# Query projections without padding, score units that include the diagonal, and a new rule for the gaps

## The chip, the cores and the metric

The kernel runs on one core of one Trainium2 chip. The metric is the time of one execution on the device in microseconds (us); the median of several executions is given. Engines are named as in the profile: PE is TensorE (PEld its weight loads), DVE is VectorE, ACT is ScalarE, POOL is GpSimd, SP is SyncE, which here only issues transfers. L401 is line 401 of the kernel before.

## The reference

One transformer layer, all in float32, with x of shape (2, 1024, 256):

```
q = x @ Wq   (16 heads of 16)        k, v = x @ Wk, x @ Wv   (4 heads of 16, each for 4 query heads)
att = softmax(q k^T / 4 + slope * (key position - query position), causal)
x = layernorm(x + (att v) @ Wo)
shared = (silu(x @ shared_gate) * (x @ shared_up)) @ shared_down
routed = one of 8 experts per row (256 -> 2 x 512 -> 256), input scaled by sigmoid(top logit)
out = layernorm(x + shared + routed)
```

## The kernel before

Rows are cut into 16 tiles of 128, eight in each batch. The four key/value heads g lie in the four quadrants of 32 partitions: kT[b] holds for head g in its 32 rows a position row, a row of ones and, from row 16 of the quadrant on, the 16 values of the head. qT[b] has the same layout for the REP = 4 query heads of a group, one after another in the free dimension, so that one matmul of 32 rows gives scores with the position term in them. In the kernel before, Wq is padded for this (`wq_pad`, 4 x 32 columns for each r): `do_q(b, r, i)` multiplies half a batch (512 columns) by one padded block for each of two r, and ScalarE adds `qbias` (the slopes, in the position rows) while it copies the result (tile `qpj`) to qT (L341).

The work before the experts goes in four stretches.

1. Start: `first_projections` turns the first half of batch 0 by transposes (`xtp0`), then projects k and v (`do_kv`: tiles kpj and vpj) and q, and turns the second half (`turn_x`, tile xtp).
2. The lead: LEAD = 10 score units run ahead of the loop, and between them `projections` puts the k, v and q of the other three halves.
3. The loop over `steps`, one for each (batch, query tile qt, key tile kt) with kt <= qt. As long as score units are left, a step has two slots. In each slot, TensorE runs a burst of four interleaved tiles: two of "t" (`t_ps`, L485: transposed scores from which ScalarE makes the probabilities pT, pD) and two of "s" (`s_ps`, L401: scores from which VectorE takes the row maximum). Behind the burst comes a gap, in which `gap(room)` may place a product (`yT`, L529), the spread of the maxima (`mT`) and the next small pieces of a finished query tile (`finish`: yq, ytp, o_ps, x1tp, lg).
4. Steps without score units have one burst and a `wide_gap`, in which a piece of the shared expert (gu_sh, dp_sh) goes too; at the end a few `last_gap`s.

A score unit covers all four g in two halves h of two quadrants, with one tile of 512 columns for each g: nr query heads times n key tiles. `s_units` gives each query tile a unit of its own for the diagonal (four heads by one key tile, four matmuls of 128 columns for each g), and units of 4, 2 or 1 key tiles for the past. In `end_s`, VectorE reduces a past tile to its maximum (L417); of a diagonal unit, VectorE takes the minimum with a causal bound for one half (L427), while ScalarE copies the other half (L435), which GpSimd masks (L438). A later reduction (L449) takes the diagonal's maximum. `maxima` joins the maxima of a query tile three slots before its first step (`join_maxima`), and one slot later transposes them into the query rows (`spread_maxima`, qS, L474).

The tiles t_ps, s_ps and all projections share six PSUM banks (`ps_st`), the small pieces and mT have one (`ps_m`), yT one. The program's order on PE, DVE, ACT and POOL is as written; SP's queue is ordered by the scheduler in this part, and as written in the experts' part. SP's transfers before the attention: x, Wo, the router, then sh_gate, sh_up and sh_down (L110 to L112) and a fill of the experts' slots in DRAM (`slot_x`, L281, 3.9 MB). The experts follow; the diff leaves them alone except for the name of the set of engines.

Of the kernel before, what the change touches and what calls it, by code (L numbers as in the profile page):

```python
# [30 lines left out]
    mybir.EngineType.DVE,  # L31
    mybir.EngineType.Activation,
    mybir.EngineType.Pool,
}


# [8 lines left out]
def attn_moe_postln_kernel(  # L45
# [61 lines left out]

    sh_gu = const.tile([P, KC, F2], F32, tag="sh_gu", name="sh_gu")
    sh_d = const.tile([P, FC, C], F32, tag="sh_d", name="sh_d")
    nc.sync.dma_start(out=sh_gu[:, :, :FF], in_=sh_gate.rearrange("(c p) f -> p c f", p=P))  # L110
    nc.sync.dma_start(out=sh_gu[:, :, FF:], in_=sh_up.rearrange("(c p) f -> p c f", p=P))
    nc.sync.dma_start(out=sh_d, in_=sh_down.rearrange("(c p) n -> p c n", p=P))  # L112

# [9 lines left out]

    wq_pad = acon.tile([P, KC, REP, N_KV, PAD], F32, tag="wq_pad", name="wq_pad")
    wk_pad = acon.tile([P, KC, N_KV, PAD], F32, tag="wk_pad", name="wk_pad")
    nc.vector.memset(wk_pad, 0.0)  # L130
    nc.vector.memset(wq_pad, 0.0)
    for c in range(KC):
        nc.vector.tensor_scalar_mul(
            wq_pad[:, c, :, :, ROW_HEAD : ROW_HEAD + HD],
            wq_raw[:, c, :].rearrange("p (g r d) -> p r g d", g=N_KV, d=HD),
            scale,
        )
        nc.vector.tensor_copy(
            wk_pad[:, c, :, ROW_HEAD : ROW_HEAD + HD],
            wk_raw[:, c, :].rearrange("p (g d) -> p g d", d=HD),  # L140
        )
# [121 lines left out]
    with (  # L263
# [11 lines left out]
    ):  # L275
        qT, kT, xT = {}, {}, {}

        empty = shp.tile([P, ROW], F32, tag="th", name="empty")
        nc.gpsimd.memset(empty, 0.0)
        nc.gpsimd.memset(empty[:, NUM : NUM + 1].bitcast(I32), NTT * P)  # L280
        nc.sync.dma_start(out=slot_xt, in_=empty.unsqueeze(1).broadcast_to([P, SLOTS // P, ROW]))  # L281


        def pj_tile(name):
            return ps_m.tile([P, 512], F32, tag="m", name=name)
# [1 line left out]
        def own_tiles(b, xTb):  # L287
            xT[b] = xTb
            kT[b] = qkp.tile([P, T], F32, tag="kT", name=f"kT_{b}")
            qT[b] = qkp.tile([P, REP, T], F32, tag="qT", name=f"qT_{b}")  # L290

        def project(dst, b, w, cols):
            for c in range(KC):
                nc.tensor.matmul(  # L294
                    dst, lhsT=w(c), rhs=xT[b][:, c, cols], start=(c == 0), stop=(c == KC - 1)
                )

        def wq_of(r):
            return lambda c: wq_pad[:, c, r].rearrange("p g d -> p (g d)")

        def wk_of(c):
            return wk_pad[:, c].rearrange("p g d -> p (g d)")
# [5 lines left out]
        def turn_x(b, i):  # L308
            if b not in xT:

                xTb = ptp.tile([P, KC, T], F32, tag="pT", name=f"xT_{b}")
                own_tiles(b, xTb)
            for c in range(KC):
                tp = bank("xtp")
                for j in range(4):
                    nc.tensor.transpose(tp[:, ts(j, P)], xs[:, b * QT + i + j, ts(c, P)], ident)
                nc.scalar.copy(xT[b][:, c, i * P : (i + 4) * P], tp)
# [15 lines left out]
                    )  # L333
            nc.scalar.copy(vs[b][:, i : i + 4, :, 0:HD], pv)

        def do_q(b, r, i):
            cols = slice(i * P, (i + 4) * P)
            for j in range(2):
                pj = bank("qpj")
                project(pj, b, wq_of(r + j), cols)  # L340
                nc.scalar.activation(qT[b][:, r + j, cols], pj, AF.Identity, bias=qbias)  # L341

        halves = [(b, i) for b in range(B) for i in range(0, QT, 4)][1:]

        def projections():


            pieces = []
            for h, after in zip(halves, [*halves[1:], None]):
                pieces.append((11, lambda h=h: do_kv(*h)))  # L350
                pieces.append((14, lambda h=h: do_q(h[0], 0, h[1])))
                if after:
                    pieces.append((4, lambda h=after: turn_x(*h)))
                pieces.append((14, lambda h=h: do_q(h[0], 2, h[1])))
            return pieces

        def first_projections():

            own_tiles(0, xTp.tile([P, KC, T], F32, tag="xT", name="xT_0"))
            cols = slice(0, 512)  # L360
            warm = bank("warm")
            zeros = mnegs[0].rearrange("p r g d -> p (r g d)")
            for i in range(2):
                nc.tensor.matmul(warm, lhsT=zeros[:, :P], rhs=zeros, start=True, stop=True)
            for c, copy in enumerate((nc.scalar.copy, nc.vector.tensor_copy)):
                tp = bank("xtp0")
                for j in range(4):
                    nc.tensor.transpose(tp[:, ts(j, P)], xs[:, j, ts(c, P)], ident)
                copy(xT[0][:, c, cols], tp)
            do_kv(0, 0)  # L370
            do_q(0, 0, 0)
            do_q(0, 2, 0)
            turn_x(*halves[0])


        def s_units(b, qt):

            units = [(0, REP, qt, 1)]
            done = 0
            while done < qt:  # L380
                n = 4 if qt - done >= 4 else 2 if qt - done >= 2 else 1
                units += [(r, 4 // n, done, n) for r in range(0, REP, 4 // n)]
                done += n
            return [(b, qt, *u) for u in units]

# [2 lines left out]
        def start_s(unit, h, j):  # L388
            b, qt, r0, nr, key, n = unit
            if (b, qt) not in rowmax:  # L390
                rowmax[b, qt] = (
                    mp.tile([P, N_KV, REP, P], F32, tag="diag", name="diag"),
                    mp.tile([P, N_KV, REP, 4], F32, tag="past", name="past", bufs=6),
                )
                parts[b, qt] = {qt: 0}
            parts[b, qt].setdefault(key, len(parts[b, qt]))
            g = h * HALF + j
            rows = slice(g * PAD, (g + 1) * PAD)
            sp = bank("s_ps")
            return sp, [  # L400
                lambda r=r: nc.tensor.matmul(  # L401
                    sp[:, r * n * P : (r + 1) * n * P],
                    lhsT=qT[b][rows, r0 + r, ts(qt, P)],
                    rhs=kT[b][rows, key * P : (key + n) * P],
                    start=True,
                    stop=True,
                )
                for r in range(nr)
            ]

        def end_s(unit, h, sp, last):
            b, qt, r0, nr, key, n = unit
            diag, past = rowmax[b, qt]
            gs = slice(h * HALF, (h + 1) * HALF)
            if key != qt:
                for j in range(HALF):
                    nc.vector.tensor_reduce(  # L417
                        past[:, h * HALF + j, r0 : r0 + nr, parts[b, qt][key]],
                        sp[j].rearrange("p (r k) -> p r k", r=nr),
                        AX.X,  # L420
                        ALU.max,
                        negate=True,
                    )
                return
            if not last:
                for j in range(HALF):
                    nc.vector.tensor_tensor(  # L427
                        diag[:, h * HALF + j],
                        sp[j].rearrange("p (r k) -> p r k", r=REP),
                        causal.unsqueeze(1).broadcast_to([P, REP, P]),  # L430
                        ALU.min,
                    )
            else:
                for j in range(HALF):
                    nc.scalar.copy(  # L435
                        diag[:, h * HALF + j].rearrange("p r k -> p (r k)"), sp[j]
                    )
                nc.gpsimd.affine_select(  # L438
                    out=diag[:, gs],
                    in_=diag[:, gs],  # L440
# [335 lines left out]
        def maxima():  # L776
            n = 0
            for k in order:
                if slot == 2 * first[k] - 3:
                    join_maxima(*k)  # L780
                if slot == 2 * first[k] - 2:
                    spread_maxima(*k)
                    n += 1
            return n
# [10 lines left out]
        def gap(room):  # L795
            nonlocal slot
            after_burst()
            start_route(True)
            if products and products[0][0] <= slot:
                product(*products.pop(0)[1])  # L800
                room -= 4
            room -= 4 * maxima()
            pieces(room)
            slot += 1

        def wide_gap():
# [6 lines left out]
            if not maxima():  # L813
                pieces(4, 4)
            slot += 1
            if tail:
                tail.pop(0)()
            after_burst()
            if not maxima():
                pieces(4, 4)  # L820
            slot += 1
# [22 lines left out]
        for k in range(LEAD):  # L844
# [5 lines left out]
            while fill and left * LEAD > total * (LEAD - 1 - k):  # L850
                left -= fill[0][0]
                fill.pop(0)[1]()
            gap(0)
        for n, (b, qt, kt) in enumerate(steps):
            last = n + 1 == len(steps) or steps[n + 1][:2] != (b, qt)
            made = []
# [40 lines left out]
    with (  # L897
# [6 lines left out]
        tc.tile_pool(name="ps_d", bufs=2, space=PSUM) as ps_d,  # L904
        tc.tile_pool(name="ps_t", bufs=2, space=PSUM) as ps_t,
        tc.tile_pool(name="rt2", bufs=1) as rtp,
        tc.manual_schedule(engines=MANUAL | {mybir.EngineType.SP}),
    ):
        wgu = wgup.tile([P, E, KC, F2], F32, tag="wgu", name="wgu")
        wd = wgup.tile([P, E, FC, C], F32, tag="wd", name="wd")  # L910
# [386 lines left out]
```

## Time and profile before

| | us |
|---|---|
| median of 6 runs | 601.69 (600.35 to 604.02) |
| the profiled execution | 603.76 |
| its span, first to last instruction | 602.0 |
| TensorE busy | 574.7 |
| VectorE busy | 343.4 |
| ScalarE busy | 267.1 |
| GpSimd busy | 155.3 |
| s_ps matmuls, L401, 1280 instructions | 185.4 |
| t_ps matmuls, L485, 576 instructions | 175.1 |
| qpj matmuls, L294, 64 instructions | 29.1 |
| mean granted TensorE clock | 0.985 |

Every fp32 matmul of the program stands as two instructions in the profile (640 score matmuls are 1280 instructions). Busy time of a group is the union of its instructions, so the four interleaved tiles of a burst count once. Matmuls in different quadrants run side by side. In the views of stretches the columns are: the stretch, its length, then for PE, PEld, DVE, ACT and POOL the busy time with the number of instructions in brackets, the granted clock, the busy share of the DMA engines and their GB/s. In a line of groups, the numbers behind the bar are busy us, mean ns of one instruction, and idle us before them with what ended it. In a timeline, they are the start and the length in us. In a line of transfers they are the KB of each and the median us from issue to landing.

### The profile page before, as it was taken

Reading aid. Unit: us, or ns where it says so; the run is one execution under the profiler, and the core shown is the slowest. Engines: PE = TensorE matmul, PEld = TensorE weight load, DVE = VectorE, ACT = ScalarE, POOL = GpSimd, SP = SyncE. Lnnn points to the kernel's source line nnn. Section 1 sums busy time; section 2 is a strip of 40 time slices with the busy share of each in tenths; the row PEclk is TensorE's granted clock in tenths of the full one; section 3 lists DMA queues with packets and bytes.
Section 4 is the critical chain, followed back from the end, with each engine's and each line's share of the span. In section 5 each row is a group of like instructions: output and inputs, shape, how many; then the busy total and the mean of one; then the engine's idle time right before and its main releaser. Section 6 shows DMA issues by size and latency. Waiting matters only on the chain. (4 is left out here: it accounts for less than half of the span.)

```text
span 602.0 us, 9431 instructions
## 1 busy us (share of the span) xinstructions
PE 574.7 (95%) x3708; PEld 329.0 (55%) x3708; DVE 343.4 (57%) x734; ACT 267.1 (44%) x484; POOL 155.3 (26%) x189
## 2 busy tenths in 40 slices
PE   8999999999999999998999999999999999999990
PEld 4555535444445353434356644545664788888650
DVE  3186767867676767777767745332551264444541
ACT  1433466665665655646575755554112111111120
POOL 4010222111110102013321220232101237766541
PEclk9999979999999999999999999999999999999996
DMA  8800000000000000000100000110153545752100
GB/s 306 249 1 2 2 0 2 1 1 1 2 2 1 1 1 0 3 0 28 45 1 1 2 1 1 35 37 1 35 203 110 176 157 180 255 180 78 46 21 4
DMA packets 23105, 32.66 MB, mean 54 GB/s; under 512 B 3295, under 2 KB 18949, under 8 KB 23057
## 3 DMA queue, kind: packets, MB, share of 16 engines
q1 hardware_dynamic: 18784, 25.28, 12.7%
q0 software_dynamic: 3456, 6.34, 3.0%
q8 instruction: 31, 0.51, 0.4%
q10 hardware_dynamic: 816, 0.39, 0.2%
q14 instruction: 18, 0.14, 0.1%
HBM read 22.20 MB, written 12.97 MB: 58 GB/s over the span
## 5 line engine op out<-in xcount | busy, mean ns | idle before, releaser
L401 PE MATMUL s_ps<-kT,qT 32*128 32x128 f32 (+2 forms) x1280 | 185.4, 380 | 1.2 <-DVE past L417 0.7
L417 DVE TENSOR_REDUCE past<-s_ps 128x1 f32<-128x512 f32 (+2 forms) x224 | 144.6, 685 | 62.6 <-PE s_ps L401 46.0
L485 PE MATMUL t_ps<-qS,kT 32*128 32x512 f32 x576 | 175.1, 642 | 0.3 <-ACT pD L507 0.3
L504 ACT ACTIVATE pT<-t_ps 128x512 f32<-128x512 f32 x224 | 121.8, 600 | 93.7 <-PE s_ps L401 65.5
L401 PEld LDWEIGHTS s_ps<-kT,qT 32*128 32x128 f32 x1280 | 96.8, 185 | 14.4 <-ACT pT L504 4.5
L485 PEld LDWEIGHTS t_ps<-qS,kT 32*128 32x128 f32 x576 | 54.0, 184 | 63.4 <-issue 23.8
L509 POOL TENSOR_SCALAR_AFFINE_SELECT pD<-pD 128x1024 f32<-128x1024 f32 x32 | 34.8, 1093 | 102.8 <-ACT pD L507 102.6
L529 PE MATMUL yT<-pT,v 128*32 128x512 f32 x448 | 59.7, 605 | 0.0
L438 POOL TENSOR_SCALAR_AFFINE_SELECT diag<-diag 128x1024 f32<-128x1024 f32 x16 | 17.5, 1094 | 135.1 <-ACT diag L435 114.4
L233 POOL TENSOR_TENSOR rstd<-rstd,neg_half 128x1 f32<-128x1 f32 x36 | 20.6, 572 | 115.4 <-DVE rstd L232 113.0
L507 ACT COPY pD<-t_ps 128x512 f32<-128x512 f32 x64 | 34.7, 601 | 24.5 <-PE s_ps L401 13.9
L688 PE MATMUL gu_sh<-x1T,sh_gu 128*128 128x512 f32 x96 | 43.5, 596 | 0.0
L239 POOL DMA_INDIRECT slot_x<-xs,slots x32 | 32.1, 1004 | 42.1 <-DVE slots L669 24.3
L449 DVE TENSOR_REDUCE past<-diag 128x8 f32<-128x1024 f32 x32 | 38.6, 1210 | 0.0
L521 ACT ACTIVATE pD<-pD 128x1024 f32<-128x1024 f32 x32 | 33.9, 1065 | 0.2 <-POOL pD L509 0.2
L1116 ACT ACTIVATE sg<-gp 128x512 f32<-128x512 f32 x16 | 9.6, 597 | 54.6 <-PE gp L1108 54.6
L1108 PE MATMUL gp<-slot_xT,wgu 128*128 128x256 f32 x128 | 30.4, 381 | 1.2 <-ACT slot_xT L1077 1.2
L1108 PE MATMUL up<-slot_xT,wgu 128*128 128x256 f32 x128 | 30.2, 379 | 0.0
L294 PE MATMUL qpj<-xT,wq_pad 128*128 128x512 f32 x64 | 29.1, 600 | 0.1
L1124 PE MATMUL dp<-wd,slot_h 128*128 128x256 f32 x128 | 29.0, 379 | 0.0
L427 DVE TENSOR_TENSOR diag<-s_ps,causal 128x512 f32<-128x512 f32 x32 | 20.5, 683 | 13.9 <-PE s_ps L401 13.9
L1053 POOL DMA_INDIRECT zt<-z_dram,row x20 | 20.7, 1033 | 27.8 <-issue 27.5
(170 smaller groups left out, 665.9 us busy)
## 6 DMA issues: line engine op xcount, KB each, us to landing
wgu<-_L_ffn_gate_up_proj_dram SPq DMA_DIRECT2D x8, 1024.0 KB, 8.8
wd<-in_L_ffn_down_proj_dram SPq DMA_DIRECT2D x8, 512.0 KB, 5.8
slot_x<-empty SPq DMA_DIRECT2D x1, 3900.0 KB
row<-slot_x SPq DMA_DIRECT2D x8, 260.0 KB, 2.9
xs<-in_L_attn_x_dram SPq DMA_DIRECT2D x4, 512.0 KB, 8.1
z_dram<-z_sh SPq DMA_DIRECT2D x12, 128.0 KB, 1.8
row<-slot_x SPq DMA_DIRECT2D x4, 130.0 KB, 2.0
sh_gu<-L_ffn_shared_gate_w_dram SPq DMA_DIRECT2D x1, 512.0 KB
```

What stands on the lines that cost most here:

```text
L239: inst = nc.gpsimd.indirect_dma_start(out=to, out_offset=bass.IndirectOffsetOnAxis(ap=index, axis=0), in_=rows, in_offset=None, bounds_che ...
L401: lambda r=r: nc.tensor.matmul(sp[:, r * n * P : (r + 1) * n * P], lhsT=qT[b][rows, r0 + r, ts(qt, P)], rhs=kT[b][rows, key * P : (key + n ...
L417: nc.vector.tensor_reduce(past[:, h * HALF + j, r0 : r0 + nr, parts[b, qt][key]], sp[j].rearrange("p (r k) -> p r k", r=nr), AX.X, ALU.max ...
L449: lambda: nc.vector.tensor_reduce(past[:, gs, :, 0], diag[:, gs], AX.X, ALU.max, negate=True),
L485: lambda: nc.tensor.matmul(tp, lhsT=kT[b][rows, ts(kt, P)], rhs=qS[b, qt][rows].rearrange("p r q -> p (r q)"), start=True, stop=True,)
L504: nc.scalar.activation(p[:, j], tp[j], AF.Exp)
L507: nc.scalar.copy(p[:, j], tp[j])
L509: nc.gpsimd.affine_select(out=p, in_=p, pattern=[[0, HALF * REP], [1, P]], compare_op=ALU.is_ge, fill=MASKED, base=0, channel_multiplier=-1,)
L521: lambda: nc.scalar.activation(p, p, AF.Exp),
L529: nc.tensor.matmul(yTs[b, qt][g * PAD : (g + 1) * PAD], lhsT=vs[b][:, kt, g, :], rhs=p[:, g, :], start=start, stop=stop,)
L688: nc.tensor.matmul(gu[k], lhsT=sh_gu[:, c, col : col + P], rhs=x1T[:, c, ts(tb, TB)], start=(c == 0), stop=(c == KC - 1),)
L1108: nc.tensor.matmul(dst[:, j], lhsT=wgu[:, e, c, col : col + P], rhs=xT[:, c, :], start=(c == 0), stop=(c == KC - 1),)
```

## The change

- Wq is no longer padded (`wq_r`). `do_q(b, i)` multiplies half a batch by two blocks of 128 columns (two r with all four g each), copies both results to a stage in SBUF (a tile of the probabilities' pool), and eight transfers of 64 KB (16 rows by 2 x 512) bring them to the head rows of qT's quadrants. Seven of the eight copies are ScalarE's and one is VectorE's. Of the 32 transfers, 28 are issued on SP, four on ScalarE's queue (the first half's, r odd).
- The other rows of qT (slopes and zeros) are written ahead of that by copies of qbias over all rows (`other_rows`), one on ScalarE and three on GpSimd, each 4 x 512 columns.
- In the first half, q is projected before k and v.
- `s_units` has no diagonal unit of its own: the last key tiles of a query tile, the diagonal included, make one group of units, which comes first. `end_s` reduces the past part of such a tile, and takes the minimum with the bound, or copies for GpSimd, on the diagonal part alone.
- `maxima` comes one slot earlier. In `gap`, a gap in which maxima are spread, or one with a product while fewer than two query tiles are being finished, has room for pieces of cost 1 only; other gaps have room 6 also beside a product; each piece now costs 4 more than its own cost. In `wide_gap`, the deferred work comes after the piece of the shared expert.
- SP's queue is in the order written. The loads of sh_gate, sh_up and sh_down and the fill of slot_x are issued after the lead.

```diff
-    wq_pad = acon.tile([P, KC, REP, N_KV, PAD], F32, tag="wq_pad", name="wq_pad")
+    wq_r = acon.tile([P, KC, REP, N_KV, HD], F32, tag="wq_r", name="wq_r")
...
+        def other_rows(b, i, copy):
+            copy(qT[b][:, :, i : i + 512], qbias.unsqueeze(2).broadcast_to([P, REP, 512]))
...
-        def do_q(b, r, i):
+        def do_q(b, i):
             cols = slice(i * P, (i + 4) * P)
-            for j in range(2):
+            stage = ptp.tile([P, N_KV, 512], F32, tag="pT", name="q_all")[:, :2]
+            for m in range(2):
                 pj = bank("qpj")
-                project(pj, b, wq_of(r + j), cols)
-                nc.scalar.activation(qT[b][:, r + j, cols], pj, AF.Identity, bias=qbias)
+                project(pj, b, wq_of(m), cols)
+                if (b, i) == (0, 0) and m == 1:
+                    nc.vector.tensor_copy(stage[:, m], pj)
+                else:
+                    nc.scalar.copy(stage[:, m], pj)
+            to = qT[b].rearrange("p (m r) t -> p r m t", r=2)
+            for r in range(2):
+                for g in range(N_KV):
+                    row = (r * N_KV + g) * HD
+                    queue = nc.scalar if (b, i, r) == (0, 0, 1) else nc.sync
+                    queue.dma_start(
+                        out=to[g * PAD + ROW_HEAD : g * PAD + ROW_HEAD + HD, r, :, cols],
+                        in_=stage[row : row + HD],
+                    )
...
-            units = [(0, REP, qt, 1)]
-            done = 0
-            while done < qt:
-                n = 4 if qt - done >= 4 else 2 if qt - done >= 2 else 1
-                units += [(r, 4 // n, done, n) for r in range(0, REP, 4 // n)]
+            units, done = [], 0
+            while done <= qt:
+                n = 4 if qt + 1 - done >= 4 else 2 if qt + 1 - done >= 2 else 1
+                units = [(r, 4 // n, done, n) for r in range(0, REP, 4 // n)] + units
                 done += n
...
+            has_diag = key + n == qt + 1
+            past_n = n - has_diag
...
+            if past_n:
                 for j in range(HALF):
                     nc.vector.tensor_reduce(
-                        past[:, h * HALF + j, r0 : r0 + nr, parts[b, qt][key]],
-                        sp[j].rearrange("p (r k) -> p r k", r=nr),
+                        past[:, h * HALF + j, heads, parts[b, qt][key]],
+                        sp[j][:, :, : past_n * P],
...
+            for j in range(HALF):
+                to, block = diag[:, h * HALF + j, heads], sp[j][:, :, past_n * P :]
+                if last:
+                    nc.scalar.copy(to, block)
+                else:
+                    bound = causal.unsqueeze(1).broadcast_to([P, nr, P])
+                    nc.vector.tensor_tensor(to, block, bound, ALU.min)
...
-                if slot == 2 * first[k] - 3:
+                if slot == 2 * first[k] - 4:
                     join_maxima(*k)
-                if slot == 2 * first[k] - 2:
+                if slot == 2 * first[k] - 3:
                     spread_maxima(*k)
...
-            if products and products[0][0] <= slot:
+            full = bool(products) and products[0][0] <= slot
+            if full:
                 product(*products.pop(0)[1])
-                room -= 4
-            room -= 4 * maxima()
-            pieces(room)
+            if maxima() or (full and len(posts) < 2):
+                room = 1
+            pieces(room, 4)
```

## The prediction

> **What bounds the kernel now.** I read the page's first line, then the busy time of each engine in five stretches (cut at the first score matmul, the end of the lead, the last score matmul, and the start of the experts), then the groups by shape, then the timeline of TensorE around single gaps.
>
> ```profile
> PE 574.7 (95%) x3708; PEld 329.0 (55%) x3708; DVE 343.4 (57%) x734; ACT 267.1 (44%) x484; POOL 155.3 (26%) x189
> ```
> ```profile
> 0.00:20.06 20.06, 17.33 (x57) 9.11 (x57) 4.56 (x16) 5.08 (x8) 6.03 (x24) 1.00 0.95 314
> 20.06:65.35 45.29, 44.60 (x351) 26.34 (x351) 28.67 (x41) 16.00 (x28) 4.37 (x4) 1.00 0.15 46
> 65.35:349.50 284.15, 279.69 (x2263) 136.57 (x2261) 207.58 (x386) 178.37 (x327) 52.34 (x54) 0.99 0.02 5
> 349.50:452.60 103.10, 101.13 (x473) 54.22 (x473) 43.65 (x124) 43.54 (x82) 20.29 (x24) 1.00 0.14 49
> ```
> TensorE is the busy engine in every stretch: 17 of 20 us at the start, 44.6 of 45.3 in the lead, 280 of 284 in the loop. That looks like a plain TensorE bound, but the loop needs a second look, because a matmul that waits inside a burst of interleaved tiles lengthens the burst and still counts as busy.
>
> ```profile
> 160.96 0.69 PE L485 MATMUL t_ps<-qS,kT 32*128 32x512 f32 x1
> ...
> 162.03 0.44 PE L594 MATMUL x1tp<-ident,xs 128*128 128x128 f32 x2
> 162.40 0.69 PE L485 MATMUL t_ps<-qS,kT 32*128 32x512 f32 x1
> ...
> 163.96 1.06 PE L529 MATMUL yT<-pT,v 128*32 128x512 f32 x8
> ...
> 196.48 0.69 PE L485 MATMUL t_ps<-qS,kT 32*128 32x512 f32 x1
> ...
> 199.48 1.06 PE L529 MATMUL yT<-pT,v 128*32 128x512 f32 x8
> ```
> A burst (two t_ps and two s_ps tiles) that waits for nothing goes from 160.96 to 162.03: 1.07. After a gap of 0.37 the next takes 162.40 to 163.96: 1.56. Two bursts with nothing between them take 196.48 to 199.48: 3.00 instead of 2.14. So a burst needs about 1 us behind it in which ScalarE and VectorE empty its PSUM banks (six banks, four per burst). A product (yT, 1.00) gives that time; a small piece does not, but costs next to nothing. Measured from the fourth t_ps instruction of one burst to that of the next, a pair "nothing, then yT" takes 3.99 where the score tile is one matmul of 512 columns and 4.34 where it is several of 128 or 256; "x1tp, then yT" takes 4.35; "nothing, then mT and yT" mostly 4.6 to 4.9. The piece beside the product costs its whole length, the piece alone almost nothing.
>
> ```profile
> L294 PE MATMUL qpj<-xT,wq_pad 128*128 128x512 f32 x64 | 29.1, 600 | 0.1
> L417 DVE TENSOR_REDUCE past<-s_ps 128x1 f32<-128x512 f32 x128 | 83.2, 685 | 36.1 <-PE s_ps L401 26.8 <-PE t_ps L485 8.8
> L427 DVE TENSOR_TENSOR diag<-s_ps,causal 128x512 f32<-128x512 f32 x32 | 20.5, 683 | 13.9 <-PE s_ps L401 13.9
> ```
>
> **The change, step by step.** The sum goes against the profiled execution's own time, 603.76 (span 602.0); the median of the runs is 601.69, 2.07 below it.
>
> *Query projection.* 64 qpj instructions become 32; 16 of them take 7.09 us in a row at the start, so 0.443 each and 14.2 in all: 3.5 before the first score, 10.6 in the lead, none later.
>
> ```profile
> 12.16 7.09 PE L294 MATMUL qpj<-xT,wq_pad 128*128 128x512 f32 x16
> ```
> *Start.* The second half of xT is copied at about 9.4, so the eight qpj instructions end at 11.3. ScalarE's new copy of qbias (2,048 elements; 0.59 for 512 and 1.07 for 1,024 make about 2.0) waits for qbias at 8.8 and ends at 10.9, the two stage copies end at 11.5 (ScalarE) and 12.0 (VectorE). Then four transfers are issued on SP (0.35 to 0.44 each in the trace) and four on ScalarE's queue (0.48 to 0.57): the last at about 14.1. Nearest landings:
>
> ```profile
> z_dram<-z_sh SPq DMA_DIRECT2D x12, 128.0 KB, 1.8
> row<-slot_x SPq DMA_DIRECT2D x4, 130.0 KB, 2.0
> ```
> So qT is there at 16.0 to 16.2. What hides it: kpj 1.82, vpj 1.73, xtp 0.97 and rps 0.1 on TensorE, until 16.0. First score at about 16.5 instead of 20.06: -3.5. Behind the four issues on ScalarE stand the copies of v and xT, which TensorE delivers only from 14.9 on. If the eight transfers landed one after another at 1.8, the first score would come at 26.5: +6.4, the other end.
> [...]
>
> *The three later halves.* Each issues eight transfers on SP, some 3.3 us of its queue, plus 2 to land; the first reader is a unit of query tile 4 or of batch 1, after the lead. Cost 0. The GpSimd copies of 2,048 (1,024 take 0.94 to 1.09, so about 2 each) precede only the fourth diag selection, wanted in loop slot 8. The loads of sh_gu and sh_d and the fill of slot_x stand behind them on SP; readers come at 352.8 and at the first routing, over 200 us on. Cost 0; uncovered it would be 5.4 MB at 314 GB/s, 17 us.
>
> *The lead.* TensorE: ten bursts of 1.08, three times kpj 1.82, vpj 1.80 and qpj 3.55, two xtp of 1.0, two mT of 0.55: 35.4. VectorE, with start-to-start times 0.62 for 512 elements and 1.14 for 1,024 (four L417 in 2.47, two L449 in 2.33), and as estimates between these and a 256-wide addition (0.42 long) 0.48, 0.35 and 0.22 for 384, 256 and 128: about 32. Two engines this close with six banks wait for each other. Following the order by hand, the third and fourth bursts, the fifth and sixth, and the eighth and ninth stand together; each pair waits 1.5 to 2, some 5 in all (in the lead of before such a pair, at 28.39, took 3.03, a wait of 0.8). So about 40 against 45.3 and one mT before: -5. Bounds: no waits, -10; VectorE carrying its whole delay into the first loop slots, -1.
>
> *Score units.* Same tiles and columns: 640 score matmuls become 448, but an unhindered burst of 128-column pieces takes 1.10 against 1.07. What counts is 4.34 against 3.99: bursts of 128 or 256 columns behind a light gap (no yT, no o_ps) fall from 23 to 17: -2. VectorE gets 32 more reductions and shorter minima (32 of 512 become 16 of 512, 16 of 256, 32 of 128): about +5 us of its time in all, in a stretch where it is 73% busy. New is that 24 units hold both past and diagonal columns. Their first tile is released after two reductions and a minimum (1.2) instead of one reduction (0.62); in the changed order, the ScalarE copies of their diagonal wait for VectorE's reductions instead of TensorE, with the next exponentials queued behind. The reductions end 0.25 to 0.5 after the two exponentials in most slots of the trace, and 384 columns save 0.27 of that, so that wait is small. 36 loop bursts are of this kind, 21 before a yT or o_ps, which hides it, 15 before a light gap: 0.2 each, +3. Bounds: 0, and 0.57 on all 36, +20.
> [...]
>
> *Gaps of the loop.* In the changed order the 124 gaps hold: mT beside yT 0 (11 before), lg beside yT 2 (7), o_ps beside yT 5 (0), gaps with nothing 13 (21). So -11 x 0.59 - 5 x 0.54 + 5 x 1.06 = -4. Bounds -9 and +2. In the wide gaps, deferred work now follows the tail piece; TensorE is 101 of 103 us busy there: 0. The experts keep their order.
>
> Sum: -3.5 - 5 - 2 + 3 - 4 = -11.5; 603.76 becomes 592.3, on the scale of the medians 590.2.
>
> **Rivals.** (a) The mixed tiles take over the pace: every mixed burst of the loop pays the 0.57, +20 instead of +3; 607. It decides from about 1 us per mixed burst spread over the 15 light gaps alone, or 0.4 on all 36 (14.5 in all instead of 3). For it: light gaps already run at the banks' pace. Against: reductions of 384 end earlier than those of 512. (b) Off TensorE's path: transfers that land one after another (first score +6.4), or a lead that stays bound by VectorE with no gain from gaps: 603.76 - 3.5 - 1 + 1 = 600.3, as a median 598; with late transfers alone, 590.2 + 9.9 = 600. The change then does less work on TensorE, and it waits instead. (c) All of it arrives: -3.5 - 10 - 2 - 9 + 0 = -24.5, as a median 577; half of what it adds, 584.
>
> **How the numbers follow.** Forecast 0.52 (its own range 585 to 597), (c) 0.13, (b) 0.17, (a) 0.18. 0.5%, 3 us, is about what a measurement of this kernel can tell from no change: faster is the forecast, (c) and a third of (b), 0.70; same 0.13; slower 0.17. Range 581 to 606: it leaves out the far end of (c) and half of (a).
>
> **What would show it.** qpj x32 at about 14.5 us busy; first score at 16 to 17 (26 if transfers queue up); the lead at 39 to 41; the loop at 279 to 283. A loop above 290 with ScalarE waiting for past would prove (a); a first score after 20 would prove (b).

## The result, and the profile after

The median went from 601.94 us (50 runs) to 597.9 us (24 runs, 596.28 to 603.24): a ratio of 0.994, interval 0.9925 to 0.9955. The direction was as forecast, but of the forecast gain of 11.5 us only 4.0 arrived. The profiled executions differ by 5.6 (603.76 to 598.12, spans 602.0 to 596.4).

The first line of the page and the first three stretches (start, lead, loop), after:

```profile
PE 559.2 (94%) x3292; PEld 308.0 (52%) x3292; DVE 346.4 (58%) x798; ACT 264.2 (44%) x508; POOL 161.1 (27%) x192
```
```profile
0.00:16.50 16.50, 13.26 (x50) 7.05 (x51) 4.46 (x16) 4.80 (x6) 7.62 (x23) 1.00 0.64 190
16.50:66.17 49.67, 43.30 (x267) 25.47 (x266) 28.25 (x55) 12.44 (x29) 6.95 (x5) 0.93 0.16 25
66.17:344.80 278.63, 270.05 (x1944) 118.74 (x1942) 211.15 (x435) 179.76 (x353) 53.72 (x57) 0.99 0.09 27
```

TensorE is busy 15.5 us less, yet the span is only 5.6 shorter. The first score does come at 16.50 instead of 20.06, but the lead then takes 49.67 instead of 45.29, at a granted clock of 0.93 instead of 1.00: it ends 0.8 later than before. The loop gives 5.5, so the gain of this execution is the loop's. The wide gaps (102.7 after, 103.1 before) and the experts (148.9, 149.4) are nearly as before.

**The start of the lead.** TensorE's timeline from the first score on, first before, then after:

```profile
20.06 0.39 PE L401 MATMUL s_ps<-kT,qT 32*128 32x128 f32 x3
20.14 0.20 PE L839 MATMUL rps<-ident,rw_raw 8*128 8x8 f32 x1
20.20 1.13 PE L401 MATMUL s_ps<-kT,qT 32*128 32x128 f32 x29
21.26 1.98 PE L294 MATMUL kpj<-xT,wk_pad 128*128 128x512 f32 x4
23.08 1.89 PE L327 MATMUL vpj<-wv_sb,xT 128*128 128x64 f32 x16
```
```profile
16.50 0.99 PE L416 MATMUL s_ps<-kT,qT 32*128 32x128 f32 x4
18.20 0.48 PE L416 MATMUL s_ps<-kT,qT 32*128 32x128 f32 x2 [0.70 <-DMA qT<-q_all]
19.10 1.93 PE L416 MATMUL s_ps<-kT,qT 32*128 32x128 f32 x26 [0.43 <-DMA qT<-q_all]
20.97 2.86 PE L291 MATMUL kpj<-xT,wk_pad 128*128 128x512 f32 x4
```

The first burst begins on time and then stands: its tiles need all eight transfers, and the last wait for one ends at 19.10. The burst takes 4.46 from its start to the next piece; before it took 1.20, and one that waits for nothing takes 1.10. Until 19.10 the matmuls are rare, and then the granted clock falls to 0.50 (half clock below). These are one-microsecond windows of TensorE (stretch, length, busy, granted clock, DMA share, GB/s):

```profile
18.00:19.00 1.00, 0.48 (x2) 1.00 0.01 0
19.00:20.00 1.00, 0.90 (x19) 0.68 0.00 0
20.00:21.00 1.00, 1.00 (x15) 0.50 0.06 16
```

Half clock holds for 3.41 us from 19.35 on, so its first 1.6 us lie inside the burst; kpj at 20.97 takes 2.70 to the next piece instead of 1.82.

**The middle of the lead.** TensorE, and below it ScalarE, around 50 us, after:

```profile
48.72 1.09 PE L315 MATMUL xtp<-ident,xs 128*128 128x128 f32 x8
52.42 2.76 PE L291 MATMUL kpj<-xT,wk_pad 128*128 128x512 f32 x4 [2.60 <-ACT xT L316]
54.98 2.81 PE L326 MATMUL vpj<-wv_sb,xT 128*128 128x64 f32 x16
```
```profile
51.20 0.67 ACT L448 COPY diag<-s_ps 128x128 f32<-128x128 f32 x2 [3.40 <-DVE past L436]
51.77 1.08 ACT L316 COPY xT<-xtp 128x512 f32<-128x512 f32 x2
```

kpj reads the xT that `xtp` has just turned. ScalarE copies it, but only behind the copies of the diagonal of a mixed score tile, and those wait 3.40 for VectorE's reductions (L436) of the same tile (a mixed tile holds past columns and diagonal columns). TensorE stands for 2.60, and half clock follows again (53.48 to 56.89). The xtp at 33.98 also has its kpj right behind it, which costs 1.3; there the copies ahead of xT are of a tile with the diagonal alone.

**The loop.** mT and a small piece in one gap, after:

```profile
89.22 0.63 PE L487 MATMUL mT<-ident,mneg 128*128 128x128 f32 x4 [0.28 <-DVE y_n L576]
91.25 0.69 PE L584 MATMUL ytp<-ident,y_n 128*128 128x128 f32 x2 [1.39 <-DVE qS L491]
```

mT and the small pieces share the one bank of `ps_m`, so ytp waits until VectorE has read mT (qS). Such a gap holds mT for 2.02 us, twice more for 1.80 (x1tp behind it), where mT alone takes 0.58. Half clock holds for 3.41 us from 91.03 on; the loop of the profiled execution before has 6.83 us of it, behind no long wait. First before, then after:

```profile
75.56:82.39 6.83, 6.83 (x28) 0.50 0.00 0
```
```profile
91.03:94.44 3.41, 3.19 (x18) 0.50 0.00 0
```

### The profile page after: what moved, and what is told of

It is laid out like the page before. It is cut to its first block, busy times and chain, and to the rows that moved or that the text cites. A ratio compares the mean times of both kernels' runs of the same rounds, so it can differ in the third digit from the quotient of the medians.

```text
span 596.4 us, 8786 instructions
## 1 busy us (share of the span) xinstructions
PE 559.2 (94%) x3292; PEld 308.0 (52%) x3292; DVE 346.4 (58%) x798; ACT 264.2 (44%) x508; POOL 161.1 (27%) x192
## 4 chain that ended last, share of the span: by engine, by line
PE 74%; DVE 9%; issue 7%; ACT 3%; DMA 2%; POOL 2%; SPq 1%; POOLq 0%; ACTq 0%; DVEq 0%
PE t_ps L502 16%; PE yT L546 10%; PE s_ps L416 10%; PE gp L1136 5%; PE dp L1152 5%; PE up L1136 5%; DVE past L436 4%; PE gu_sh L705 3%; PE dp_sh L725 2%; PE o_ps L591 2%; PE qpj L291 2%; DVE past L466 1%; PE kpj L291 1%; PE dp L1194 1%; PE gp L1044 1%
## 5 line engine op out<-in xcount | busy, mean ns | idle before, releaser
L416 PE MATMUL s_ps<-kT,qT 32*128 32x512 f32 (+2 forms) x896 | 188.3, 476 | 3.2 <-DMA qT<-q_all 1.1
L436 DVE TENSOR_REDUCE past<-s_ps 128x1 f32<-128x512 f32 (+3 forms) x256 | 147.9, 618 | 65.2 <-PE s_ps L416 49.2
L502 PE MATMUL t_ps<-qS,kT 32*128 32x512 f32 x576 | 167.0, 641 | 0.3 <-ACT pD L524 0.3
L416 PEld LDWEIGHTS s_ps<-kT,qT 32*128 32x128 f32 x896 | 83.3, 188 | 19.2 <-DVE past L436 7.2
L502 PEld LDWEIGHTS t_ps<-qS,kT 32*128 32x128 f32 x576 | 49.9, 183 | 62.1 <-issue 30.9
L448 ACT COPY diag<-s_ps 128x128 f32<-128x128 f32 (+2 forms) x64 | 21.7, 385 | 20.4 <-DVE past L436 15.8
L451 DVE TENSOR_TENSOR diag<-s_ps,causal 128x128 f32<-128x128 f32 (+2 forms) x64 | 23.9, 414 | 7.7 <-PE s_ps L416 7.6
```

Of the source, the lines that this page charges most:

```text
L416: lambda r=r: nc.tensor.matmul(sp[:, r * n * P : (r + 1) * n * P], lhsT=qT[b][rows, r0 + r, ts(qt, P)], rhs=kT[b][rows, key * P : (key + n ...
L436: nc.vector.tensor_reduce(past[:, h * HALF + j, heads, parts[b, qt][key]], sp[j][:, :, : past_n * P], AX.X, ALU.max, negate=True,)
L502: lambda: nc.tensor.matmul(tp, lhsT=kT[b][rows, ts(kt, P)], rhs=qS[b, qt][rows].rearrange("p r q -> p (r q)"), start=True, stop=True,)
```

## The experiments

Theory: the query projection is worth what was forecast, but its landing and the places of xtp and kpj in the lead take it back, with half clock behind each wait; mixed score tiles make the second of these worse; and mT with a piece takes back part of the gaps. Rivals: the parts are worth less than forecast in themselves (mixed tiles slow the loop), or a low clock alone explains the loss. Differences between kernels are of medians; taken from the ratios to the kernel before, which ran beside each, they differ by up to 0.7, for the matmuls on zeros by 1.5. The mark "first loop burst" below is the fourth t_ps instruction, 68.35 before and 68.12 after; "loop" is from there over 124 slots, 281.63 before and 276.67 after.

**The second half's k and v ahead of the first scores.** Edits are against the changed kernel unless said otherwise. This fills the time until the transfers land. It changes the order behind that too: at the two later places a score burst now stands between xtp and the kpj that reads its result.

```diff
-                pieces.append((14, lambda h=h: do_kv(*h)))
+                if h != halves[0]:
+                    pieces.append((14, lambda h=h: do_kv(*h)))
...
             turn_x(*halves[0])
+            do_kv(*halves[0])
```


> The changed kernel with the k and v projection of the second half placed ahead of the first score unit instead of behind it. Theory: the first burst waited from 16.5 to 19.1 for the transfers of q; 3.6 us of other work covers that wait and the half clock behind it (1.7): 593 to 595 us. Rival: kpj waits for ScalarE's copies of xT instead, which stand behind four transfers' issues, and the wait only changes its name: 597 to 598 us.

Measured: 589.4, ratio 0.9806 (0.9785 to 0.9826), 8.5 below the changed kernel. TensorE's timeline of this kernel where the wait was and around the first of the two later places, and the stretch from there to the end of the lead:

```profile
16.65 1.98 PE L291 MATMUL kpj<-xT,wk_pad 128*128 128x512 f32 x4 [0.24 <-ACT xT L316]
18.47 1.90 PE L326 MATMUL vpj<-wv_sb,xT 128*128 128x64 f32 x16
...
20.44 1.13 PE L418 MATMUL s_ps<-kT,qT 32*128 32x128 f32 x29
...
26.21 1.09 PE L315 MATMUL xtp<-ident,xs 128*128 128x128 f32 x8
27.53 2.43 PE L418 MATMUL s_ps<-kT,qT 32*128 32x256 f32 x16 [0.23 <-DVE diag L453]
29.90 1.98 PE L291 MATMUL kpj<-xT,wk_pad 128*128 128x512 f32 x4
```
```profile
16.65:56.79 40.14, 39.47 (x266) 22.60 (x267) 28.08 (x55) 12.27 (x28) 6.95 (x5) 1.00 0.20 30
```

The burst takes 1.20 undisturbed, no wait behind an xtp is longer than 0.35, the clock stays at 1.00, and the lead takes 40.1; what is left of waits lies inside bursts (2.37 for the one at 27.53). The work that TensorE does is the same; only its order differs. The time is some 4 us below the 593 to 595 that I had expected: I had counted the first wait alone, and this edit mends the places behind xtp as well. It doesn't tell the two apart.

**Matmuls on zeros in the wait.** Three extra matmuls of 512 columns of zeros run before the first score and change no output; they keep TensorE busy while the transfers land.

```diff
+        idle = pj_tile("idle")
+        zeros = mnegs[0].rearrange("p r g d -> p (r g d)")
+        for i in range(3):
+            nc.tensor.matmul(idle, lhsT=zeros[:, :P], rhs=zeros, start=True, stop=True)
```


> The changed kernel with three matmuls of zeros (2.7 us) that fill the wait for the first transfers. Nothing useful is added. Theory: the wait itself costs 2.6 us, and another 1.7 are lost because the clock is at half for 3.4 us behind it; with TensorE kept busy the first burst ends at about 20.2 instead of 21.0 and kpj takes 1.82 instead of 2.70: 596 to 596.5 us. Rival: the clock has no part, kpj is slow for another reason: 598 us or above.

```profile
16.97 2.84 PE L862 MATMUL idle<-mneg 128*128 128x512 f32 x6 [0.27 <-DVE rwT L858]
19.74 1.17 PE L416 MATMUL s_ps<-kT,qT 32*128 32x128 f32 x32
20.84 1.98 PE L291 MATMUL kpj<-xT,wk_pad 128*128 128x512 f32 x4
```

The zeros end at 19.74, 0.6 behind the last wait of the changed kernel, so the burst ends at 20.84 and not at the expected 20.2. That is as late as in the changed kernel (20.97), but no half clock follows and kpj takes its 1.82. In this execution (595.08, the shortest of the 12) the wait at 50 us brought none either, and the lead ends at 63.52, 2.65 before that of the changed kernel: that is what half clock cost there. The median, 596.6 (12 runs; ratio 0.9943, interval 0.9918 to 0.9969), can't be told from the changed kernel's. So in the trace the clock is a part of the loss, and 7 us to the forecast end of the lead (56.5) are left without it.

**All eight transfers on SP's queue.**

```diff
-                    queue = nc.scalar if (b, i, r) == (0, 0, 1) else nc.sync
+                    queue = nc.sync
```


> All eight transfers of the first half's q are issued on SP instead of four on SP and four on ScalarE's queue; nothing else is changed. This tells whether the start is set by how long the issues take one behind another on a queue. Theory (serial issue at 0.59 each on SP): the issues run from about 12.9 to 17.7 instead of 15.8, the last transfer lands at about 20 to 21 instead of 18 to 19, and the first score burst, which still begins at about 16.5, ends about 1.8 later than the 21.0 of the changed kernel; TensorE waits in it for about 5 us and not 3.4. Rival 1 (a transfer's flight of 2.3 to 3.8 sets the start, and issues overlap whatever the queue): the end stays within 0.5 of 21.0. Rival 2 (ScalarE's queue is what is late, because its issues take 0.71 and stand behind its copies): the end comes earlier, about 20. The single time is expected within 2 us of the changed kernel, so it is the trace that answers.

Windows of TensorE with the DMA share and GB/s in the last two columns, first the changed kernel, then this one:

```profile
15.00:16.00 1.00, 1.00 (x11) 1.00 0.93 207
16.00:17.00 1.00, 0.96 (x8) 1.00 1.13 148
```
```profile
15.00:16.00 1.00, 1.00 (x11) 1.00 0.69 107
16.00:17.00 1.00, 1.00 (x12) 1.00 0.63 105
```

This kernel ran once, and none of the three expectations is met whole. The issues run to 18.1 instead of 15.8, but the last wait ends at 19.90, only 0.8 later, and the burst is over at 20.76. That lies within the 0.5 of 21.0 that the first rival named, though not for its reason: the waits are short and spread, and no half clock lengthens the burst. With one queue the issues set the pace: 64 KB each 0.59 us is 111 GB/s, and 98 to 107 are moved. With two queues the 16 DMA engines are full for two of the four microseconds (0.93 and 1.13 of their time), which speaks against a gain from issuing still faster; that was not tried. Serial issue alone, as I had it, falls. The 2.60 wait at 50 us is there too, and this time half clock lasted 13.65 behind it; the time was 601.48.

**Turning x ahead of the q pieces**, so that qpj and not kpj stands behind xtp:

```diff
-                pieces.append((14, lambda h=h: do_q(*h)))
                 if after:
                     pieces.append((4, lambda h=after: turn_x(*h)))
+                pieces.append((14, lambda h=h: do_q(*h)))
```


> The changed kernel with the next half's turn (xtp) ahead of the q projection again, so that qpj (3.6 us) stands between xtp and the kpj that reads its result. Theory: in the changed lead, kpj waits 1.3 and 2.75 us for ScalarE's copies of xT right behind xtp, and the second wait brings a stretch of half clock (1.7 us lost). Both go: 592 to 594 us, no stretch of half clock near 53 us. Rival: the lead is bound by VectorE and the banks, so the waits only move to the score bursts: 597 to 598 us.

597.17, ratio 0.9935 (0.9919 to 0.9951): no different, as the rival had it. Much of the wait only changed its name. The xtp at 44.30 is followed by qpj, which needs a bank and waits 1.90 for VectorE's reductions (L436); the piece takes 2.99 instead of 3.70. The first loop burst is at 66.04, 2.1 earlier, with as much half clock ahead of it (one stretch of 6.83 instead of two of 3.41); in the loop a second stretch of 3.41 takes most of that back. As a test of the adjacency it is inconclusive; the next one touches the cause itself.

**ScalarE's copy ahead of VectorE's reductions**, in the lead only:

```diff
+            copied = has_diag and last and slot < 0
+            if copied:
+                for j in range(HALF):
+                    nc.scalar.copy(diag[:, h * HALF + j, heads], sp[j][:, :, past_n * P :])
...
-                if last:
+                if last and not copied:
                     nc.scalar.copy(to, block)
-                else:
+                elif not last:
```


> The changed kernel where, in the lead alone, ScalarE copies the diagonal part of a mixed tile before VectorE reduces its past part, so that ScalarE waits for TensorE and VectorE for ScalarE. Theory: in the changed lead, ScalarE's copies of xT (for which kpj waits) stand behind diagonal copies that wait for VectorE, which lags; with the order turned the xtp at 48.7 is followed by kpj after about 2 us instead of 3.7, and the half clock behind it may go: lead 2 to 4 us shorter, 594 to 596 us. Rival: kpj waits because it stands directly behind xtp, and ScalarE's order has no part: 597 to 598 us.

593.11 (7 runs), ratio 0.9854 (0.9827 to 0.988), 4.8 below the changed kernel. ScalarE's timeline of this kernel, and TensorE's kpj behind the same xtp:

```profile
50.49 0.43 ACT L437 COPY diag<-s_ps 128x128 f32<-128x128 f32 x2 [1.02 <-PE s_ps L416]
51.09 1.07 ACT L316 COPY xT<-xtp 128x512 f32<-128x512 f32 x2 [0.16 <-PE xtp L315]
```
```profile
52.28 1.95 PE L291 MATMUL kpj<-xT,wk_pad 128*128 128x512 f32 x4 [0.79 <-ACT xT L316]
```

The diagonal copy waits for TensorE (1.02) and no more for VectorE (3.40). kpj waits 0.79 instead of 2.60, and no half clock follows it. Only the order of two readers of one bank was changed: the queue of ScalarE behind VectorE is shown to be a cause. Its size is the wait that went: the first loop burst is at 66.30, 1.8 earlier, with as much half clock ahead of it (one stretch of 6.83 behind the first burst). The profiled execution took 597.22 with that and two stretches in the loop, at a mean clock of 0.980; five of the other six took 592.4 to 593.2 at 0.989. So the rest of the 4.8 seems to go with the clock, but no kept trace shows where.

**No piece beside mT.**

```diff
-            if maxima() or (full and len(posts) < 2):
+            if maxima():
+                room = 0
+            elif full and len(posts) < 2:
                 room = 1
```


> The changed kernel with no small piece in a gap that spreads maxima. Theory: mT, x1tp and ytp share one PSUM bank, so a piece behind mT in the same gap waits for VectorE's qS addition; these three gaps took 3.2, 3.2 and 4.8 us against 1.9 for mT alone, and the last one brought a stretch of half clock. Gone, and the pieces cost up to 0.6 each elsewhere: 593 to 595 us. Rival: the pieces land beside products at their own length and nothing is won: 597 to 599 us.

591.36, ratio 0.984 (0.9822 to 0.9859), 6.5 below the changed kernel, where I had expected 593 to 595. TensorE's timeline at the same place: the next burst starts 0.56 behind mT.

```profile
89.69 0.63 PE L487 MATMUL mT<-ident,mneg 128*128 128x128 f32 x4 [0.28 <-DVE y_n L576]
90.25 0.69 PE L502 MATMUL t_ps<-qS,kT 32*128 32x512 f32 x1
```

The loop takes 270.21 instead of 276.67. Three gaps lose 1.44, 1.22 and 1.22 of waiting, and the half clock at the first (91.03 to 94.44) goes, worth 1.7 if half of it counts as lost. The 0.9 that are left are not traced to single waits.

**The parts alone**, on the kernel before: the gap rules; the score units together with these; and the query part (`wq_r`, `do_q`, `other_rows`, the transfers and the later loads).

```diff
 # the gap rules alone
-                if slot == 2 * first[k] - 3:
+                if slot == 2 * first[k] - 4:
                     join_maxima(*k)
...
+            if maxima() or (full and len(posts) < 2):
+                room = 1
+            pieces(room, 4)
 # and with the units
-            units = [(0, REP, qt, 1)]
+            units, done = [], 0
 # the query part alone
-                project(pj, b, wq_of(r + j), cols)
+                project(pj, b, wq_of(m), cols)
```


> The kernel before with the gap rules alone changed (maxima one slot earlier, room, deferred work behind the tail piece). Theory: this is where the loop's 5 us come from, less than it could be because mT and a piece on its bank stand in one gap in some places: 597 to 600 us. Rival: the shorter loop comes from the score units with fewer pieces, and the gap rules alone give 600 to 602 us.

> The changed kernel with the query projection put back (padded, no transfers): new score units and gap rules, old projections. Theory: the lead stays at before's length or a little over (10.6 us of qpj come back, the waits go), the loop keeps its gain: 596 to 599 us, about the changed kernel's time, since the projection as it stands brings almost nothing. Rival: the projection brings its 14 us and the rest loses 10: 608 us or above.

> The kernel before with the query projection alone changed (unpadded, by transfers, with SP's order and the moved loads); score units and gap rules are as before. Theory: the lead loses what it gains, whatever the units: the wait for the transfers (2.6), xtp directly ahead of kpj, and half clock behind such waits; but ScalarE's copies no longer wait for VectorE there, so the waits in front of kpj are shorter: first loop burst 2 to 5 us earlier than before, 597 to 600 us. Rival: the score units are what spoils the lead, and without them the 10.6 us come through: 590 to 592 us.

| on the kernel before (601.47 in these runs) | median of 12 | ratio (95%) | first loop burst | loop |
|---|---|---|---|---|
| gap rules | 598.92 | 0.9956 (0.9938 to 0.9973) | 68.13 | 277.73 |
| gap rules and units | 601.99 | 1.0004 (0.9987 to 1.0021) | 69.78 | 276.51 |
| query part | 599.29 | 0.9955 (0.9928 to 0.9982) | 63.09 | 279.42 |

The gap rules bring 2.5, the units take 3.1 of it back, and the query part on top of both brings the 4.1 that are left. Alone, the query part brings 2.2 in the median, though its profiled execution (595.57, at the low end of 595.4 to 603.34) shows the first loop burst 5.3 earlier and no half clock ahead of it. Its clock tells the runs apart: the three at 0.992 took 595.4 to 595.7, the nine at 0.979 to 0.987 took 598.8 to 603.3. Gap rules and units came to 601.99, neither the 596 to 599 that I expected nor the 608 of the rival. The units cost 1.65 of the lead with the old projection; with the new one and the gap rules together 5.0 (63.09 to 68.12), of which 2.5 is half clock that the query part's execution did not have and 0.3 the end of the first burst. In the loop, with the old projection, they win 1.2 (277.73 to 276.51, each with one stretch of half clock). The remaining difference of the medians is in no kept trace. With the units of before, kpj waits behind xtp as well (2.89 and 1.78 from xtp to kpj, where xtp is 1.0 long): the places of xtp and kpj make this wait, and the units lengthen it at the second place and shorten it at the first.

**The repairs together**, and then with the units taken out or the copies turned:

```diff
 # the two repairs: k and v ahead, no piece beside mT (as above)
 # then, of these, the units of before
-            units, done = [], 0
+            units = [(0, REP, qt, 1)]
 # or the copies turned in the lead
+            copied = has_diag and last and slot < 0
```


> Both repairs at once: k and v of the second half ahead of the first score unit, and no piece beside mT. If the two losses are separate they add up: 597.9 - 6.5 - 8.5 = 583; if both saved the same thing (the half clock near 91 us), 586 to 588 us.

> Both repairs (585.4 us together), but with the score units of before: the diagonal as a unit of its own. Theory: the new units cost 1.5 to 3 us (with the old projections, 602.0 with them and 598.9 without), most of it in the lead: 582 to 584 us. Rival: the units were spoiled by the lead's waits only, which the repairs removed, and in the loop they gain about 1: 586 to 587 us.

> Both repairs and, in the lead, ScalarE's diagonal copies ahead of VectorE's reductions. Theory: what is left of waits in the repaired lead (bursts of 2.1 to 2.4 us beside xtp, some 3 us in all) comes in part from that order: 583 to 584.5 us. Rival: with other work between xtp and kpj the order costs nothing any more, 585 to 586 us.

| | median of 5 | ratio to before (95%) | first loop burst | loop |
|---|---|---|---|---|
| both repairs | 585.43 | 0.973 (0.9703 to 0.9757) | 58.95 | 272.99 |
| and the units of before | 581.74 | 0.967 (0.9644 to 0.9696) | 57.41 | 271.16 |
| and the copies turned | 581.58 | 0.9677 (0.9649 to 0.9705) | 58.02 | 270.19 |

The repairs nearly add up (8.5 and 6.5 would give 582.9; 585.43 lies between the two expectations). On the repaired kernel the units again cost 3.6 by the ratios (0.973 to 0.967). In the traces 1.5 of it is in the lead and 1.8 in the loop, and 1.7 of the latter is one stretch of half clock, which only the kernel with both repairs has:

```profile
66.70:70.11 3.41, 3.41 (x16) 0.50 0.98 308
```

With the copies turned in the lead the units cost nothing that can be told. Both last kernels beat the kernel before by over 3%, the second of them with the change's own matmuls.

## Why the prediction was right or wrong

The prediction failed in the stretch from the start to the end of the lead. Its two terms, -3.5 and -5, should have ended the lead 8.5 earlier; it ended 0.8 later. The loop's sum, -3, came out near its size.

**Work on TensorE: right.** qpj x32 is 15.1 us busy, with 14.5 forecast; the 448 score matmuls are there, as 896 instructions; and the busy time fell by 15.5.

**The start, -3.5: wrong, about -0.3 at the end of the first burst.** The first score came at 16.50 as forecast, but the step "qT is there at 16.0 to 16.2" failed; the last wait for a transfer ended at 19.10. The first burst therefore ended at 20.97, as against 21.26 before. Three sizes were off: VectorE's copy to the stage ended at 12.83 and not 12.0; an issue took 0.59 on SP and 0.71 on ScalarE's queue (medians of this execution), where I had taken 0.35 to 0.57 from rows of other transfers; and the landing that the profile gives for the four SP transfers is 3.8, against 1.8 to 2.0 (the median over all 28 issued on SP is 2.3), while the two queues kept the DMA engines full (0.93 and 1.13 of their time): from the end of the last issue to the end of the last wait it was 3.3 with two queues and 1.8 with one. I had also named the wrong sign: the first score came at 16.50 with transfers still to land (the last wait ended at 19.10), so "a first score after 20" could not show late transfers; the end of the first burst does.

**The lead, -5: wrong, +4.4.** This counts from the first score, so the late landing, which the start had taken as done, is in it. My own sum was 35.4 of work and 5 of waits for banks. The trace has 35.2 (one of the two mT lies behind the stretch) and 4.5: this part was right. Beside it stand 3.4 of landing (some 0.8 of which is half clock inside the first burst), 1.3 and 2.75 of waits of kpj behind xtp, and 2.5 of half clock behind the waits (0.88, 0.74 and 0.92): 35.2 + 4.5 + 9.95 is 49.65, beside the 49.67 measured. The failing step is that I summed each engine's work and the bank waits, but not what stands in ScalarE's queue between an xtp and the kpj that reads it. I had noted that ScalarE's diagonal copies now wait for VectorE "with the next exponentials queued behind", and looked for it in the loop; in the lead it is the copy of xT that is queued. I had also put half clock at nothing. With k and v ahead, which mends the landing and both places, the lead took 40.1, the 40 of the forecast, and the time was 589.4 beside the 590.2 forecast.

**Units, +1 in all: too low, +3.1 to +3.6 by the medians.** The +1 was meant for the loop, and there the traces show no more: -1.2 with the old projection, +0.1 on the repaired kernel without the half clock. What I left out is the lead, where the units cost 1.5 to 2.2 in all three pairs. There the two readers of a mixed tile stood one behind the other: ScalarE's copy waited 3.40 for VectorE's reductions. I had priced that wait of the copies in the loop, at 0.2, and not the queue behind them in the lead: turning the order of the two readers there is worth 3.2 on the repaired kernel (0.973 to 0.9677), half clock included.

**Gaps, -4: too large, -2.5 alone.** The count of gap kinds was right: the trace after has 0, 2, 5 and 13 of those that I counted. What I did not price is mT with a small piece on one bank: without these three gaps the changed kernel is 6.5 faster.

**The loop, -3: right.** 281.63 went to 276.67, by 5.0; but 3.4 of the 281.63 is a half-clock stretch of 6.83 in the profiled execution of before, and 1.7 of the 276.67 one of 3.41, if half of each counts as lost. Without both it is -3.3. The sum is nearer than its parts, and that is luck: I had the gaps win too much and the units cost too much. This also tells why the profiled executions differ by more than the medians.

**The later transfers and moved loads, 0: right.** TensorE's matmuls wait for qT<-q_all only at the start (1.1), and the wide gaps and experts kept their lengths.

**The rivals.** (a) falls: the loop is at 279 by the stretches, not above 290. (b) is the one that came, in its core "it waits instead", with 0.17 given to it. That its 598 meets the 597.9 measured is chance, since the causes I gave are not those that came: the transfers were late by 3 us and not by 10, since they overlap, and the lead was not bound by VectorE's work (busy 28 of 50 us) but by who stands behind VectorE in ScalarE's queue. (c) falls with the lead.

## What to carry to other kernels

When work is taken off the busiest engine in a stretch ordered by hand, follow each in-order queue through the new order: a piece that reads what its neighbour has just produced pays for everything queued on the engine between the two. Put independent work between the issue of a transfer and its first reader until the measured landing is covered, counting issue times on each queue and how full the DMA engines get. Here two tiles that share one bank did not belong in one gap (6.5 us less without that), and of two engines that read one bank the one whose queue was needed next had to read first (kpj then waited 0.79 instead of 2.60). And compare the granted clock of two executions before reading a difference of 2 us as one of the kernels: a stretch of half clock of 3.41 us was worth 1.7, an estimate that counts half of it as lost.

## What the runs showed of the hardware

- Up to the experts, TensorE's granted clock fell to 0.50 in stretches of 3.41 us (changed kernel, from 19.35, 53.48 and 91.03), 6.83 (kernel before, from 75.56) and 13.65 (one queue). It often came with a wait: at the 2.60 in the lead in three of four traces (3.41 in the changed kernel and with no piece beside mT, 13.65 with one queue, none with the matmuls on zeros), and in the first burst, with 1.2 to 1.4 us of idling, in four of five (not in the query part alone, with 1.3). In the loop of the changed kernel it came at the 1.39 between mT and ytp, and not at the 1.14 between mT and x1tp (161.67). It also came without one: at 75.56 in the kernel before, with 0.31 us of idling in the 3.41 ahead of it. So these runs give no length of wait that decides it.
- Issuing a 64 KB transfer from SBUF to SBUF took 0.59 us on SP alone. With two queues issuing at once the medians were 0.59 on SP and 0.71 on ScalarE's queue in the changed kernel. One queue moved 98 to 107 GB/s and two up to 207, with the DMA engines busy for 0.93 and 1.13 of their time: a second queue ended the last wait 0.8 us sooner (19.10 and 19.90).
